# A second handover in each layer 1 step, and priority for the pre-pass softmax statistics

## The chip, the cores and the metric

The kernel runs on one core of one Trainium2 chip. The metric is the device time of one execution in microseconds; 4537.07 us is the median of three runs before the change (4530.45 to 4539.39). The core's engines each work through their own queue in order: TensorE (PE for matmuls, PEld for weight loads), VectorE (DVE), ScalarE (ACT), GpSimd (POOL) and SyncE (SP, which here only issues transfers).

## The reference

Four images of 32 x 32 positions and 384 channels pass through four layers; each adds its result to its input after a group normalisation (32 groups of 12 channels). N is 1024 positions.

```python
x = x + L0(_gn(x), ...)   # deformable attention, 6 heads of 64
x = x + L1(_gn(x), ...)   # attention with grouped weights, 12 heads of 32
x = x + L2(_gn(x))        # box sums over x and channels, a quotient
x = x + L3(_gn(x), ...)   # outlook attention, 3 x 3 windows

# L0: q = x @ w_q; offsets from a grouped 3 x 3 convolution of q, layer norm, gelu, tanh
xs = _bilinear_sample(xg, pos)                    # x at the offset positions
attn = softmax(einsum(q, xs @ w_k) * scale + bilinear(rpe, disp))
out = einsum(attn, xs @ w_v) @ w_out

# L1: per head, n and m over the 1024 positions
sim = sigmoid(beta + alpha * einsum('bhnd,bhmd->bhnm', l2norm(xg_h), l2norm(gc)))  # m: 256
group_weight = einsum('bhnm,bhkm->bhnk', sim, sim) * gamma + (1.0 - gamma)
attn = softmax(einsum('bhnd,bhmd->bhnm', q, k) * scale, axis=-1) * group_weight
attn = attn / (attn.sum(axis=2, keepdims=True) + 1e-08)      # sum over the rows n
out = einsum('bhnm,bhmd->bhnd', attn, v) @ Wproj
```

In layer 1 the softmax normalises over m and the second division sums over n. The kernel works on transposed scores, so it needs each row's logarithm of the softmax sum (maximum plus the log of the sum of exponentials) before it makes the scores. These logarithms come from a pre-pass.

## The kernel before

Two lanes of work are traced into one program. The trunk takes an image through layers 1, 2 and 3; the front takes the next image through layer 0. Both are Python generators that hand over with `yield w`, where w is a number of work units: 1109 for an image of the trunk, 714 for an image of the front. `Net.layer3` (L286) draws them: after each yield of the trunk it adds w / 1109 to what is done, and then draws from the front until the front is 0.1 of an image ahead. So a trunk yield of 14 draws 9.01 front units on the average, in whole pieces. Layer 0 of image 0 runs by itself ahead of this, and beside image 3 of the trunk no front is left.

The order in which the pieces are traced is a priority only. When the tile context closes, a scheduler goes through the program in modelled time, and whenever an engine is free it issues, of the instructions that are ready by its model, the one with the earliest place in the trace. `high_priority()` moves the places of what is traced inside it to the front, and `issue_after(ins)` keeps a block's instructions of one engine behind `ins`. The order on each engine is then fixed. On the chip an engine waits at its next instruction until that is ready, whatever stands behind.

**Layer 1 (trunk).** `inputs1` (L1198) makes the projections, the group convolution and the norms, and the pre-pass of head pair 0. Then `pair(p)` (L1463) handles six pairs of heads, each in eight steps j over 128 columns. A step scales a slice of sim on GpSimd (`sg`, L1513); makes the scores of 128 by 1024 for both heads in two double banks (L1530) and their exponentials (L1538, tiles `e`); then four products `product(h, r)`: the group weights of half h and head r, by transposing blocks that were kept from earlier steps (L1555) and by matmuls of sg and sim (L1560), multiplied into `e` with a running sum on VectorE (L1567), with a copy of the blocks wanted later (L1572). `values` (L1490), one step late, divides by the sums and adds to the value product `av` (L1502), a bank that is held for the whole pair. The first two or three products (`parts[:split]`) stand ahead of a piece of the next pair's pre-pass, the others behind.

**The pre-pass.** `sums_step(i, st)` (L1388) multiplies queries by keys into two double banks (L1397), takes the negative maximum on VectorE (L1405) and the exponential with its sum on ScalarE (L1406). Eight such steps make a pair's statistics; `sums_log` (L1414) turns them into the logarithm with two Newton steps (L1423 to L1429), and `sums_row` (L1432) transposes it (L1436) and stores it. In a pair's step the pre-pass matmuls stand behind the last product's matmul by `issue_after`.

**Layer 0 (front).** For each of six heads and two halves of the queries, `head0` (L831) has four key pairs (`yield 6` each): gathers of bias windows by GpSimd transfers (L845), interpolation on ScalarE and VectorE (L857, L858, L862, L863), two logits matmuls into two banks (L869), their sum with the bias (L872) and a running maximum (L874, L876). Then the maximum is transposed, reduced and spread (L883 to L895, `yield 3`), and eight keys follow in four pairs (`yield 2` each): subtraction (L902), exponential (L903), and matmuls with the values and with ones (L905). A copy and a store end the half (`yield 3`), and `over_sums` (L1127) divides after every second head.

All PSUM tiles come from two pools: `ps2` with two double banks (`big`), used by scores, pre-pass and sims, and `ps1` with four banks (`bank`), used by products, values, logits and the attention sums of layer 0.

Of the kernel before, what the change touches and what calls it, by code (L numbers as in the profile page):

```python
# [19 lines left out]
I32 = mybir.dt.int32  # L20
AF = mybir.ActivationFunctionType
ALU = mybir.AluOpType
AX = mybir.AxisListType
# [1127 lines left out]
class Trunk(Lane):  # L1151
# [236 lines left out]
    def sums_step(self, i, st):  # L1388

        nc, v = self.nc, self.nc.vector  # L1390
        nmax, den = st
        ps = [self.big() for _ in range(2)]
        for h in range(2):
            for r in range(2):
                c = 2 * h + r
                rows = slice(HD1 * c, HD1 * (c + 1))
                nc.tensor.matmul(  # L1397
                    ps[r][:, h * 512 : (h + 1) * 512],
                    self.q4[rows, i * P : (i + 1) * P],
                    self.k4[rows, 0:512],  # L1400
                    start=True,
                    stop=True,
                )
        for r in range(2):
            v.tensor_reduce(nmax[:, r, i : i + 1], ps[r], AX.X, ALU.max, negate=True)  # L1405
            nc.scalar.activation(  # L1406
                ps[r],
                ps[r],
                AF.Exp,
                bias=nmax[:, r, i : i + 1],  # L1410
                accum_out=den[:, r, i : i + 1],
            )

    def sums_log(self, st):  # L1414

        nc, v = self.nc, self.nc.vector
        nmax, den = st


        d = self.wt([P, 2, NJ], "dsum")  # L1420
        e = self.wt([P, 2, NJ], "dexp")
        ln2 = float(np.log(2.0))
        v.tensor_copy(d, den.bitcast(I32))  # L1423
        v.tensor_scalar(d, d, ln2 / 2**23, -(127.0 - 0.043) * ln2, ALU.mult, ALU.add)
        for _ in range(2):
            nc.scalar.activation(e, d, AF.Exp, scale=-1.0)
            v.tensor_tensor(e, e, den, ALU.mult)
            v.scalar_tensor_tensor(d, e, -1.0, d, ALU.add, ALU.add)
        v.tensor_tensor(d, nmax, d, ALU.subtract)  # L1429
        return d  # L1430

    def sums_row(self, p, d):  # L1432
# [30 lines left out]
    def pair(self, p):  # L1463
# [3 lines left out]
        nc, v = self.nc, self.nc.vector  # L1467
# [22 lines left out]
        def values(j, es, tot):  # L1490

            rt = self.wt([P, 2], "rt", 2)
            v.scalar_tensor_tensor(rt, tot[:, :, 0], 1e-8, tot[:, :, 1], ALU.add, ALU.add)
            v.reciprocal(rt, rt)
            vs = self.wt([P, 2, HD1], "vs", 2)
            v.tensor_tensor(  # L1496
                vs, vn[:, j].rearrange("p (r c) -> p r c", r=2), bc(rt, 2, HD1), ALU.mult
            )
            for h in range(2):
                for r in range(2):  # L1500
                    r0 = HD1 * (2 * h + r)
                    nc.tensor.matmul(  # L1502
                        av[r0 : r0 + HD1, :],
                        vs[:, r, :],
                        es[h][:, r, :],
                        start=j == 0,
                        stop=j == NJ - 1,
                    )

        for j in range(NJ):  # L1510
# [14 lines left out]
            for h in range(2):  # L1525
                cols = slice(h * 512, (h + 1) * 512)
                ps = self.big().rearrange("p (r n) -> p r n", r=2)
# [9 lines left out]
                e = self.wt([P, 2, 512], "e", 4)  # L1537
# [41 lines left out]
            with self.tc.issue_after(last):  # L1579
                if st and j < 2:  # L1580
                    self.sums_step(2 * j, st)
                elif st and j < 6:
                    self.sums_step(j + 2, st)
                elif st and j == 6:
                    self.sums_row(p + 1, logs)
                    self.load_lse(p + 1)
                    self.sims(0)
            for h, r in parts[split:]:
                last = product(h, r)
            with self.tc.issue_after(last):  # L1590
# [7 lines left out]
            if st and j == 5:  # L1598
                logs = self.sums_log(st)
                if p + 2 < NH1 // 2:  # L1600
                    self.load_sums(p + 2)
            yield 14
        values(*late.pop())
        y = self.wt([P, 512], "y")
        nc.scalar.copy(y, av)
# [357 lines left out]
```

## Time and profile before

| what | value |
|---|---|
| median of three runs | 4537.07 us (4530.45 to 4539.39) |
| profiled execution, its own time | 4529.22 us |
| its span, first to last instruction | 4527.0 us |
| mean granted TensorE clock | 0.932 |
| TensorE matmuls busy | 4011.3 us, 89% |
| VectorE / ScalarE / GpSimd busy | 3128.7 / 2308.8 / 960.1 us |
| pre-pass maximum, L1405 | 384 of 1219 ns |
| pre-pass exponential, L1406 | 384 of 1089 ns |
| product on VectorE, L1567 | 768 of 748 ns |

Times within the trace are microseconds from the start of the span. Each group line gives the busy time and the mean duration of one instruction, then the idle time of the engine ahead of it and what ended that. A waits line such as "PE bank L869 <- ACT gn L1572" says that TensorE stood still at line 869, which writes a tile `bank`, until ScalarE's instruction of line 1572 was done; the numbers are the total, the count and the longest. A row of the windows view has the stretch, its length, the busy time of PE, PEld, DVE, ACT and POOL with instruction counts, the granted clock, the share of the DMA engines and GB/s. A row of the timeline has start, duration, engine, line and operation.

By the trace, image 0's layer 0 runs up to about 560 us. The pair stages of images 0 to 3 lie at about 812 to 1440, 1916 to 2545, 3022 to 3658 and 3930 to 4310 us.

### The profile page before, as it was taken

To read this page: it belongs to the slowest core of one execution; us is meant where nothing else is said; L and a number is where in the kernel's file an instruction comes from. 1 tells how busy PE (TensorE), PEld (TensorE's weight loads), DVE (VectorE), ACT (ScalarE), POOL (GpSimd) and SP (SyncE) were. 2 spreads that over 40 slices of the span, in tenths; PEclk is the share of its full clock that TensorE was granted. 3 is DMA by queue.
4 is the path that set the end of the run, shared out by engine and by line. 5 is a ranking of instruction groups with operands and counts; after the bars stand their busy time and mean duration, and the time that the engine had idled before them with its cause. 6 is when DMAs were issued, how large, how long until landed. Compare 5 with 4: busy or idle time off the path is not lost.

```text
span 4527.0 us, 47048 instructions
## 1 busy us (share of the span) xinstructions
PE 4011.3 (89%) x15672; PEld 1702.4 (38%) x15672; DVE 3128.7 (69%) x5925; ACT 2308.8 (51%) x3633; POOL 960.1 (21%) x970
## 2 busy tenths in 40 slices
PE   5589889989899897998899989789999998999998
PEld 2222334333334443333333344343333334344444
DVE  3599566878887627677888744667788874566654
ACT  2176334666665323556766423456566651466632
POOL 0655123212121104211212110422121311000000
PEclk8799998999999898999999989898999998999998
DMA  7445344222222255312222135431122213311011
GB/s 153 146 148 145 100 129 120 75 57 77 62 66 63 82 134 151 111 48 58 85 58 82 38 95 154 143 107 51 45 78 58 78 38 115 121 29 37 22 41 42
DMA packets 298322, 389.85 MB, mean 86 GB/s; under 512 B 167875, under 2 KB 229664, under 8 KB 298080
## 3 DMA queue, kind: packets, MB, share of 16 engines
q1 hardware_dynamic: 246040, 220.14, 17.8%
q0 software_dynamic: 39936, 145.53, 10.9%
q10 hardware_dynamic: 12104, 21.19, 1.4%
q8 instruction: 124, 2.03, 0.2%
q14 instruction: 118, 0.97, 0.1%
HBM read 300.48 MB, written 86.56 MB: 85 GB/s over the span
## 4 chain that ended last, share of the span: by engine, by line
PE 57%; DVE 20%; issue 8%; ACT 5%; DMA 5%; POOL 3%; SPq 1%; another core or an unknown queue 0%; ACTq 0%; DVEq 0%; POOLq 0%
PE bank L1560 12%; PE big L1530 6%; PE big L400 5%; PE bank L905 4%; PE bank L414 4%; PE big L1397 4%; PE bank L1502 3%; DVE nmax L1405 3%; PE bank L1555 2%; PE bank L869 2%; DVE e L1567 2%; PE big L665 2%; DVE lg L872 2%; PE bank L1235 2%; PE big L1700 2%
## 5 line engine op out<-in xcount | busy, mean ns | idle before, releaser
L1560 PE MATMUL bank<-whole,sg 128*128 128x512 f32 (+3 forms) x2304 | 838.5, 497 | 0.0
L1567 DVE SCALAR_TENSOR_TENSOR e<-bank,gam,e 128x512 f32<-128x512 f32 x768 | 560.3, 748 | 298.6 <-PE bank L1560 146.8
L1406 ACT ACTIVATE big<-big,nmax 128x1024 f32<-128x1024 f32 x384 | 418.2, 1089 | 283.7 <-DVE nmax L1405 275.5
L1538 ACT ACTIVATE e<-big 128x1024 f32<-128x1024 f32 x384 | 380.5, 1020 | 289.3 <-PE big L1530 283.3
L1560 PEld LDWEIGHTS bank<-whole,sg 128*128 128x128 f32 x2304 | 396.3, 194 | 342.6 <-issue 254.3
L1405 DVE TENSOR_REDUCE nmax<-big 128x1 f32<-128x1024 f32 x384 | 453.1, 1219 | 85.7 <-PE big L1397 51.2
L1530 PE MATMUL big<-qa,ka 64*128 64x512 f32 x1536 | 463.2, 653 | 28.0 <-ACT big L1406 27.1
L845 POOL DMA_INDIRECT win<-strips,widx x288 | 326.8, 1135 | 714.6 <-DVE z L858 346.7
L1513 POOL TENSOR_SCALAR sg<-whole,gam 128x512 f32<-128x512 f32 x192 | 146.9, 766 | 1303.6 <-PE bank L1560 1029.0
L1397 PE MATMUL big<-k,q 32*128 32x512 f32 x1536 | 289.4, 662 | 47.7 <-ACT big L1406 35.0
L737 POOL DMA_INDIRECT gat<-pairs,sidx x192 | 207.8, 1082 | 408.1 <-DVE ix_gt L515 209.0
L905 PE MATMUL bank<-lg,va 128*64 128x512 f32 x576 | 271.3, 618 | 20.8 <-ACT lg L903 20.7
L905 PE MATMUL bank<-lg,ones 128*64 128x512 f32 x576 | 270.7, 618 | 0.0
L1530 PEld LDWEIGHTS big<-qa,ka 64*128 64x128 f32 x1536 | 164.3, 197 | 262.5 <-issue 111.3
L863 DVE SCALAR_TENSOR_TENSOR lg<-z,bias_f,lg 128x512 f32<-128x512 f32 x288 | 219.6, 778 | 62.4 <-ACT lg L862 58.4
L1502 PE MATMUL bank<-e,vs 128*32 128x512 f32 x1536 | 239.5, 632 | 6.6 <-DVE vs L1496 6.5
L857 ACT ACTIVATE z<-win,bias_f 128x528 f32<-128x528 f32 x288 | 204.5, 738 | 51.0 <-DMA win<-strips,widx 26.7
L858 DVE SCALAR_TENSOR_TENSOR z<-win,bias_f,z 128x528 f32<-128x528 f32 x288 | 216.7, 770 | 8.9 <-issue 4.6
L872 DVE TENSOR_TENSOR lg<-bank,lg 128x512 f32<-128x512 f32 x288 | 192.5, 684 | 35.4 <-PE bank L869 35.4
L862 ACT ACTIVATE lg<-z,bias_f 128x512 f32<-128x512 f32 x288 | 201.0, 719 | 18.4 <-DVE z L858 10.3
L902 DVE TENSOR_TENSOR lg<-lg,tb 128x512 f32<-128x512 f32 x288 | 183.8, 694 | 38.1 <-ACT tb L895 38.1
L903 ACT ACTIVATE lg<-lg 128x512 f32<-128x512 f32 x288 | 170.6, 628 | 44.8 <-DVE lg L902 41.6
(314 smaller groups left out, 6673.5 us busy)
## 6 DMA issues: line engine op xcount, KB each, us to landing
pairs<-xn SPq DMA_DIRECT2D x64, 192.0 KB
q<-qd SPq DMA_DIRECT2D x48, 256.0 KB
xg<-xgd SPq DMA_DIRECT2D x48, 256.0 KB
w<-in_gmat SPq DMA_DIRECT2D x16, 576.0 KB
w<-in_w_off SPq DMA_DIRECT2D x12, 576.0 KB
w<-in_Wqkv SPq DMA_DIRECT2D x12, 576.0 KB
a<-in_x SPq DMA_DIRECT2D x16, 384.0 KB
x<-a ACTq DMA_DIRECT2D x4, 1536.0 KB
```

The source lines that it names most:

```text
L400: nc.tensor.matmul(ps[:, h * 512 : (h + 1) * 512], w[:, ki, lo + ko * P : lo + (ko + 1) * P], mov, start=ki == 0, stop=ki == KC - 1,)
L845: nc.gpsimd.indirect_dma_start(out=win, out_offset=None, in_=self.strips[:, :], in_offset=bass.IndirectOffsetOnAxis(ap=self.widx[:, q, c : ...
L872: v.tensor_tensor(lf, ps[u], lf, ALU.add)
L905: nc.tensor.matmul(po[out, :], w, lf, start=j == 0, stop=j == NJ - 1)
L1397: nc.tensor.matmul(ps[r][:, h * 512 : (h + 1) * 512], self.q4[rows, i * P : (i + 1) * P], self.k4[rows, 0:512], start=True, stop=True,)
L1405: v.tensor_reduce(nmax[:, r, i : i + 1], ps[r], AX.X, ALU.max, negate=True)
L1406: nc.scalar.activation(ps[r], ps[r], AF.Exp, bias=nmax[:, r, i : i + 1], accum_out=den[:, r, i : i + 1],)
L1502: nc.tensor.matmul(av[r0 : r0 + HD1, :], vs[:, r, :], es[h][:, r, :], start=j == 0, stop=j == NJ - 1,)
L1530: nc.tensor.matmul(ps[:, r, :], ka[rows, j * P : (j + 1) * P], qa[rows, cols], start=True, stop=True,)
L1538: nc.scalar.activation(e, ps, AF.Exp)
L1560: last = nc.tensor.matmul(ps[:, (mid - i0) * P :], sg[:, r, m, :], sim[:, h, r, m, (mid - i0) * P :], start=m == 0, stop=m == 1,)
L1567: v.scalar_tensor_tensor(e[:, r, :], ps, self.gam[:, 1:2], e[:, r, :], ALU.add, ALU.mult, accum_out=tot[:, r, h : h + 1],)
```

## The change

Each step of `pair` yields 7 units twice in place of 14 once. The new yield stands behind the first products and the pre-pass piece that follows them, ahead of the remaining products. The pre-pass maximum and exponential of `sums_step` and all of `sums_log` are traced under `high_priority()`; the pre-pass matmuls are not. The instructions are the same.

```diff
         for r in range(2):
-            v.tensor_reduce(nmax[:, r, i : i + 1], ps[r], AX.X, ALU.max, negate=True)
-            nc.scalar.activation(
-                ps[r],
-                ps[r],
-                AF.Exp,
-                bias=nmax[:, r, i : i + 1],
-                accum_out=den[:, r, i : i + 1],
-            )
+            with self.tc.high_priority():
+                v.tensor_reduce(nmax[:, r, i : i + 1], ps[r], AX.X, ALU.max, negate=True)
+                nc.scalar.activation(
+                    ps[r],
+                    ps[r],
+                    AF.Exp,
+                    bias=nmax[:, r, i : i + 1],
+                    accum_out=den[:, r, i : i + 1],
+                )
...
-        v.tensor_copy(d, den.bitcast(I32))
-        v.tensor_scalar(d, d, ln2 / 2**23, -(127.0 - 0.043) * ln2, ALU.mult, ALU.add)
-        for _ in range(2):
-            nc.scalar.activation(e, d, AF.Exp, scale=-1.0)
-            v.tensor_tensor(e, e, den, ALU.mult)
-            v.scalar_tensor_tensor(d, e, -1.0, d, ALU.add, ALU.add)
-        v.tensor_tensor(d, nmax, d, ALU.subtract)
+        with self.tc.high_priority():
+            v.tensor_copy(d, den.bitcast(I32))
+            v.tensor_scalar(d, d, ln2 / 2**23, -(127.0 - 0.043) * ln2, ALU.mult, ALU.add)
+            for _ in range(2):
+                nc.scalar.activation(e, d, AF.Exp, scale=-1.0)
+                v.tensor_tensor(e, e, den, ALU.mult)
+                v.scalar_tensor_tensor(d, e, -1.0, d, ALU.add, ALU.add)
+            v.tensor_tensor(d, nmax, d, ALU.subtract)
         return d
...
+            yield 7
             for h, r in parts[split:]:
                 last = product(h, r)
             with self.tc.issue_after(last):
...
-            yield 14
+            yield 7
         values(*late.pop())
```

## The prediction

> **What bounds the kernel now.** I read the page from the top: the span and the busy shares, then the forty slices, then single stages in the windows view, then TensorE's waits in one stage, and last the timeline at one wait.
>
> ```profile
> span 4527.0 us, 47048 instructions
> PE 4011.3 (89%) x15672; PEld 1702.4 (38%) x15672; DVE 3128.7 (69%) x5925; ACT 2308.8 (51%) x3633; POOL 960.1 (21%) x970
> PE   5589889989899897998899989789999998999998
> DVE  3599566878887627677888744667788874566654
> PEclk8799998999999898999999989898999998999998
> ```
>
> TensorE is the bound, 89% of the span over all. The windows view sets the pair stage of images 0, 1 and 2, which runs beside layer 0 of the next image, against that of image 3, which runs alone (last line):
>
> ```profile
> 812.00:1440.00 628.00, 573.17 (x2415) 231.10 (x2417) 510.46 (x1017) 399.04 (x634) 133.00 (x130) 0.96 0.23 65
> 1916.00:2545.00 629.00, 573.89 (x2413) 230.94 (x2409) 510.56 (x1016) 399.41 (x634) 132.50 (x130) 0.96 0.23 65
> 3022.00:3658.00 636.00, 583.16 (x2419) 234.60 (x2415) 511.37 (x1017) 399.11 (x634) 131.62 (x130) 0.94 0.23 65
> 3930.00:4310.00 380.00, 375.15 (x1757) 156.88 (x1755) 246.88 (x560) 238.63 (x377) 28.12 (x40) 1.00 0.13 34
> ```
>
> Alone, TensorE idles 4.9 of 380 us at full clock. Beside layer 0 it idles 55.1 of 629 us (54.8 and 52.8 in the other two) at a mean clock of 0.94 to 0.96, while VectorE is 81% busy. All that the change can win is in these three stretches and the stage ahead of each. Who holds TensorE there (image 1, pair stage and the run-in; total, times, longest):
>
> ```profile
> PE bank L883 <- DVE rmax L876: 11.4, 8, 1.7
> PE big L1530 <- ACT big L1406: 8.5, 3, 3.2
> PE big L1397 <- ACT big L1406: 6.5, 4, 2.7
> PE bank L1555 <- DVE lg L872: 5.2, 6, 2.1
> PE bank L869 <- ACT gn L1572: 5.0, 3, 3.6
> PE bank L905 <- ACT lg L903: 4.5, 3, 2.1
> PE bank L869 <- DVE lg L872: 3.9, 4, 2.7
> ```
>
> Two causes stand out. One is the pre-pass (L1406): its two double banks are all that the scores also use. The timeline shows why it is late; the product L1397 ends at 1980.67, its maximum starts only at 1983.62, behind layer 0's L858 and L863:
>
> ```profile
> 1978.36 2.31 PE L1397 MATMUL big<-k,q 32*128 32x512 f32 x8
> 1980.14 1.45 DVE L858 SCALAR_TENSOR_TENSOR z<-win,bias_f,z 128x528 f32<-128x528 f32 x2
> 1982.29 1.42 DVE L863 SCALAR_TENSOR_TENSOR lg<-z,bias_f,lg 128x512 f32<-128x512 f32 x2
> 1983.62 2.35 DVE L1405 TENSOR_REDUCE nmax<-big 128x1 f32<-128x1024 f32 x2
> 1986.94 3.18 PE L1397 MATMUL big<-k,q 32*128 32x512 f32 x8 [2.64 <-ACT big L1406]
> ```
>
> The other is layer 0's seam L876, L883, where its running maximum is turned. And a stall costs twice; in the windows behind the one above the clock (third column from the end) is halved for 6.83 us, then whole again:
>
> ```profile
> 1986.35:1993.18 6.83, 6.24 (x20) 1.97 (x21) 6.05 (x12) 4.40 (x9) 4.59 (x4) 0.50 0.29 91
> 1993.18:2000.01 6.83, 6.83 (x30) 3.41 (x32) 5.62 (x10) 2.84 (x5) 0.00 (x0) 1.00 0.17 47
> ```
>
> **The change part by part.** No instruction is added or removed; the scheduler's order changes.
>
> *A, priority of maximum and exponential.* In image 1 (1860 to 2545 us) I read off the timeline, for each of the pre-pass steps, the time from the end of L1397 to the start of L1405: 14 of 36 wait over 0.6 us, 35.8 us together, longest 5.21. TensorE's waits that follow are 8.5 + 6.5 for L1406, and the 3.6 of L869 behind the copy L1572, which stood behind two exponentials: 18.6 us, so 0.52 us of stall per us of delay. Near them lie 23.9 us at half clock, worth up to 12 us; 0.64 us per us of stall. With priority the maximum waits only for the instruction under way (about 0.4 us), and the 18.6 us should go. What is late next is the VectorE work passed by: 14 times two reduces of 1.22 us, 34 us. Of the 60 instructions ahead of the late maxima, 13 are the trunk's own L1567, which free banks; 47 are layer 0's. If only the trunk's hurt, at the same 0.52, 3.9 us come back; if all do, 17.8. I take the middle, 10.8, since layer 0's L902 feeds L905, whose wait is in the list above, while L858 only fills logits tiles ahead of need. Net 7.8 us, 12.8 with the clock, 38 over three images. Ends: 18.6 x 1.64 x 3 = 92 won; all 34 us come back, 15.6 x 1.64 x 3 = 77 lost. ScalarE is 63% busy here and I cost its reordering within these ends.
>
> The clock's share can be weighed against the Trainium skill, "TensorE: Matmul & The Clock Gate", section "HAM oscillation", which says that only idle gaps over about 3.4 us throttle. By that rule no stall of this stage but the 3.6 us one would cost clock; the row above (0.50 after 2.64 us) says otherwise, and the sum goes by the row.
>
> *B, the seam.* Counting both generators' yields: a step of 14 trunk units draws 9.01 of layer 0 (14 x 714 / 1109). A key pair's block is 6 (call it L), the turn of the maximum 3 (X), a pair of exponentials with L905 2 (A). Before, 6 of an image's 7 X came in one handover right behind their last L, and 11 times two L came together; with 4.5 units per half step neither happens at all. Half a step of trunk matmuls (629 / 48 = 13.1 us a step) then stands between L876 and L883. Reach: 11.4 us x 6/7, with 6.8 us of clock likewise, 15.6 us an image, 47 in all. I take half, 23, because the scheduler places by readiness and not by trace order alone. Against it, 26 of the 38 A now come half a step nearer to X; L905's wait was 2.07 us each time, and two more of them per image cost 12 (ends 0 and six, 37). Net 11 won.
>
> *C, the mid-step blocks.* 27 of the 44 L in an image's pair stage move ahead of the step's last one or two products. An L holds two of four banks until L872, and the value product holds one throughout, so the products behind it share one. TensorE's waits behind L872 are 3.9 + 5.2 us per image now, 0.21 per L; I charge that again for the 27: 17 in all. Ends: nothing, and a whole L1567 and copy (0.75 + 0.37 us) each time, 27 x 1.12 x 3 = 91. I stay near the row that shows the same wait at its present place.
>
> *The queues.* Each moved L carries two POOL gathers (L845), four ScalarE scalings and two key loads per head on SP. The next step's L1513 stands behind both handovers before and after, so POOL's order to the trunk is kept, and POOL is 21% busy there. On SP the blocks of j = 5, with the sums' loads and stores of layer 0, move ahead of the four loads of load_sums; these are wanted two steps, 26 us, later. Nothing is charged; without that slack a rden load (4.2 us in the chain) would be the price.
>
> *D, the logarithm.* Its tiny chain (0.17 us each) makes TensorE wait 5.7 + 3.4 us at L1436 over 24 pairs; I take 4 back.
>
> *E, the stage before the pairs.* The pre-pass of pair 0 stands behind layer 0's gather weights (L750), with TensorE waiting 5.3 + 1.1 us for L1406 an image: up to 19 to win. Pushing L753 back by three steps of 2.44 us would cost as much at L764: 22. I take nothing.
>
> Image 3 has no layer 0 left and its maxima start 0.04 us after their products: nothing. Sum: -38 - 11 + 17 - 4 = -36. The profiled execution took 4529.2 us (span 4527.0 and 2.2 around it), so 4493; the median of the runs shown is 7.9 above it, so 4501.
>
> **The rivals.**
>
> *The banks decide (slower).* C at its upper end, 91 in place of 17: -38 - 11 - 4 + 91 = +38, 4575. It turns from 0.65 us per moved block on. For it: the 3.6 us wait at L869 was one for a bank. Against it: single waits behind L872 are rarely over 1 us. Beside it, the same sign by another place: *the passed VectorE work comes back in full*, decided where over 0.54 us returns per us passed; at 0.7, 18.6 - 23.9 = -5.3, +26, and with the rest 4565. Its measured neighbour, 0.52, is close, which is why I don't give it little. Together 0.28.
>
> *The priority moves nothing.* The scheduler may hold the product for unfinished where the hardware has it done, and then no maximum is ready to go ahead. A and D are nothing, -11 + 17 = +6: 4543, within what can be told. Speaking for it: nothing in the trace shows what the scheduler believed. Against: L902, three in a row, is all ready at once, and the maximum stands behind it in six of the 14. 0.10.
>
> *Stalls vanish without a return.* A at 92, B at 47, D at 9 and C at 17: 4406; half way there 4454. For it: image 3. Against: VectorE's 81%. 0.08.
>
> *Idle costs no clock.* A 23, B 15 less 12, C 17, D 4: -13, 4524. The rows at 0.50 speak against it. 0.04. By the rule of the Trainium skill above this would be the time.
>
> **How the numbers follow.** The forecast keeps 0.50 (4470 to 4527 by itself). A measurement of this kernel tells 0.2% (9 us; its three runs lie 8.9 apart). Faster: 0.50 + 0.08 + 0.04 = 0.62; same 0.10; slower 0.28. The range runs from 4445, which leaves out part of the no-return case, to 4572, which takes in the returned work and stops just short of the banks' end.
>
> **What would show it.** A right: the gap from L1397 to L1405 falls under 0.5 us beside layer 0, and "L1397 <- L1406" and "L1530 <- L1406" nearly go from TensorE's waits. B right: "L883 <- L876" falls to a few us an image. C: waits of L1555, L1560 or L869 for L872 and L1567 grow by about 6 us an image. D: L1436 no longer waits for L1429. The pair windows' idle goes from 55 to some 45 us and the clock toward 0.98. It would be wrong if L1567 and L902, passed by, left TensorE as idle as before under other names, or if the mid-step blocks starve the products of banks.

## The result and the profile after

The changed kernel takes 4498.34 us (median of six runs, 4493.76 to 4509.69), the kernel before 4533.61 us on the same chip: a ratio of 0.993, 95% interval 0.9913 to 0.9947. The forecast was 4501 us. The number came out; most of the working behind it did not.

The page of the changed kernel, in the lines shown of before (its profiled execution took 4504.37 us, mean clock 0.937 after 0.932):

```profile
span 4502.6 us, 47093 instructions
PE 3953.3 (88%) x15672; PEld 1661.2 (37%) x15672; DVE 3108.4 (69%) x5925; ACT 2305.0 (51%) x3633; POOL 949.3 (21%) x970
PE   5589898898989798899899989798989998999998
PEclk8799998999999898999999989899999998999998
```

TensorE is busy 58 us less, with the same number of instructions, in a span that is 24.4 us shorter. So it stands still longer than before and yet finishes earlier. The prediction had said that its idle time would go.

The windows view, with the whole pair stage of images 0 to 2 (first to last score product) in a row each. Before:

```profile
713.00:1431.00 718.00, 659.61 (x2687) 267.24 (x2687) 567.60 (x1106) 450.06 (x718) 157.89 (x155) 0.96 0.24 69
1818.00:2537.00 719.00, 657.29 (x2690) 266.54 (x2689) 569.48 (x1108) 450.94 (x718) 155.75 (x153) 0.96 0.25 70
2921.00:3647.00 726.00, 666.28 (x2688) 270.10 (x2686) 569.31 (x1106) 450.65 (x718) 157.83 (x155) 0.95 0.25 69
```

and after:

```profile
725.00:1435.00 710.00, 642.33 (x2689) 255.01 (x2688) 565.28 (x1112) 450.61 (x719) 153.10 (x155) 0.97 0.25 70
1814.00:2534.00 720.00, 656.14 (x2686) 260.00 (x2685) 565.03 (x1112) 450.12 (x718) 151.12 (x152) 0.95 0.24 68
2916.00:3627.00 711.00, 642.18 (x2687) 254.74 (x2686) 564.60 (x1112) 449.19 (x719) 149.91 (x152) 0.97 0.24 69
```

To a tenth, the three stages beside layer 0 took 718.0, 718.7 and 725.8 us before and now take 709.5, 720.4 and 711.3. That is 21.3 of the 24.4 us. Image 3, alone, is as it was (443.0, now 442.7). Idle in the three grew from 58.4, 61.7 and 59.7 us to 67.7, 63.9 and 68.8, while time at half clock fell from 61.6, 58.0 and 78.7 us to 44.9, 72.8 and 42.7. Image 1 has more half-clock time than before, and it is the one stage that gained nothing.

TensorE's waits in the pair stage of image 1 (lines from L1405 on stand one or two lower down in this kernel: L1405 is L1406, L1406 is L1407, L1496 is L1498, L1502 is L1504, L1530 is L1532, L1555 is L1557, L1567 is L1569):

```profile
PE big L1532 <- ACT big L1407: 24.6, 12, 5.1
PE bank L891 <- POOL diag L889: 7.8, 9, 1.3
PE bank L1557 <- DVE lg L872: 5.5, 5, 2.3
PE bank L1504 <- DVE vs L1498: 5.5, 5, 1.9
PE bank L869 <- DVE e L1569: 5.1, 5, 2.2
...
PE bank L883 <- DVE rmax L876: 1.7, 2, 1.4
```

The seam L883 went from 11.4 to 1.7 us. But the wait that the priority was to remove did not go: 8.5 us at the scores and 6.5 at the pre-pass products became 24.6 at the scores. The page's groups show the other half of it. Before:

```profile
L1530 PE MATMUL big<-qa,ka 64*128 64x512 f32 x1536 | 463.2, 653 | 28.0 <-ACT big L1406 27.1 <-issue 0.3
L1397 PE MATMUL big<-k,q 32*128 32x512 f32 x1536 | 289.4, 662 | 47.7 <-ACT big L1406 35.0 <-ACT e L1538 8.5 <-issue 3.8
L1502 PE MATMUL bank<-e,vs 128*32 128x512 f32 x1536 | 239.5, 632 | 6.6 <-DVE vs L1496 6.5
```

and after:

```profile
L1532 PE MATMUL big<-qa,ka 64*128 64x512 f32 x1536 | 453.0, 672 | 84.2 <-ACT big L1407 79.3 <-ACT e L1540 2.2 <-issue 1.6
L1397 PE MATMUL big<-k,q 32*128 32x512 f32 x1536 | 263.8, 658 | 65.2 <-ACT big L1407 48.4 <-ACT e L1540 11.8 <-issue 4.9
L1504 PE MATMUL bank<-e,vs 128*32 128x512 f32 x1536 | 207.9, 608 | 18.2 <-DVE vs L1498 18.2
```

The scores wait 79.3 us in place of 27.1. The value products take 207.9 us busy in place of 239.5, and the pre-pass products 263.8 in place of 289.4, at nearly the same mean duration of one. Such products run side by side, so busy time that falls at an equal mean means that more of them overlap.

Why did the priority not pull the maximum forward? The timeline of the changed kernel at its longest wait, the 5.09 us one:

```profile
2212.56 1.14 PE L1397 MATMUL big<-k,q 32*128 32x512 f32 x8
...
2213.55 0.08 DVE L1569 DVE_READ_ACCUMULATOR e<-bank,gam,e 128x1 f32 x1
2214.50 1.13 DVE L863 SCALAR_TENSOR_TENSOR lg<-z,bias_f,lg 128x512 f32<-128x512 f32 x1 [0.87 <-issue]
2215.55 0.76 DVE L858 SCALAR_TENSOR_TENSOR z<-win,bias_f,z 128x528 f32<-128x528 f32 x1
2216.23 0.74 DVE L1569 SCALAR_TENSOR_TENSOR e<-bank,gam,e 128x512 f32<-128x512 f32 x1
...
2218.39 0.74 DVE L858 SCALAR_TENSOR_TENSOR z<-win,bias_f,z 128x528 f32<-128x528 f32 x1
2219.06 2.34 DVE L1406 TENSOR_REDUCE nmax<-big 128x1 f32<-128x1024 f32 x2
...
2221.56 1.23 PE L1532 MATMUL big<-qa,ka 64*128 64x512 f32 x2 [5.09 <-ACT big L1407]
```

The product is done at 2213.70. VectorE stands idle for 0.87 us until 2214.50, and L863, L858, the trunk's L1569 and more go first; the maximum, which has the priority, starts 5.36 us after its product. VectorE's 5157 instructions start in this trace in exactly the order in which the program queues them, so the maximum's place was set by the scheduler. Over the 40 pre-pass steps of image 1's stage the mean gap from product to maximum rose from 0.96 to 1.22 us, and 19 of them wait over 0.6 us where 14 did.

The gap alone doesn't make the longer wait, though. Here is a step in which the maximum is prompt, 0.47 us after its product (2108.79):

```profile
2107.65 1.14 PE L1397 MATMUL big<-k,q 32*128 32x512 f32 x8
...
2108.72 1.07 PE L1504 MATMUL bank<-e,vs 128*32 128x512 f32 x8
...
2109.26 2.35 DVE L1406 TENSOR_REDUCE nmax<-big 128x1 f32<-128x1024 f32 x2
...
2111.83 1.83 PE L1532 MATMUL big<-qa,ka 64*128 64x512 f32 x6 [0.98 <-ACT big L1407]
```

From the start of the maximum to the scores it takes 2.57 us, for one maximum and one exponential, and TensorE had only 2.06 us of other work. So such a wait is the gap plus about 2.6 us, less the work that TensorE has between the pre-pass product and the scores. For the 12 waits in image 1's stage that is 27.6 + 30.8 - 33.4 = 25.0 us, and 24.6 were measured; for the three of before, 12.2 + 7.7 - 11.1 = 8.8 against 8.5. Before, each of the 40 steps had at least 2.6 us of work there; now 7 have less. That, besides the longer gaps, is why the wait grew.

### The profile page after: what moved, and what is told of

It reads as the page before. It is cut to its first block, busy times and chain, and to the rows that moved or that the text cites. A ratio compares the mean times of both kernels' runs of the same rounds, so it can differ in the third digit from the quotient of the medians.

```text
span 4502.6 us, 47093 instructions
## 1 busy us (share of the span) xinstructions
PE 3953.3 (88%) x15672; PEld 1661.2 (37%) x15672; DVE 3108.4 (69%) x5925; ACT 2305.0 (51%) x3633; POOL 949.3 (21%) x970
## 3 DMA queue, kind: packets, MB, share of 16 engines
q0 software_dynamic: 39936, 145.53, 10.8%
## 4 chain that ended last, share of the span: by engine, by line
PE 53%; DVE 22%; issue 9%; ACT 7%; DMA 4%; POOL 3%; SPq 1%; another core or an unknown queue 1%; ACTq 0%; DVEq 0%; POOLq 0%
PE bank L1562 11%; PE big L1532 6%; PE big L400 5%; PE bank L905 4%; DVE nmax L1406 4%; PE bank L414 4%; PE big L1397 3%; DVE e L1569 3%; ACT big L1407 3%; PE bank L1557 2%; PE big L665 2%; PE bank L1235 2%; PE bank L1504 2%; PE bank L869 2%; DVE lg L872 2%
## 5 line engine op out<-in xcount | busy, mean ns | idle before, releaser
L1562 PE MATMUL bank<-whole,sg 128*128 128x512 f32 (+3 forms) x2304 | 853.9, 501 | 1.5
L1569 DVE SCALAR_TENSOR_TENSOR e<-bank,gam,e 128x512 f32<-128x512 f32 x768 | 560.3, 746 | 314.2 <-PE bank L1562 184.8
L1407 ACT ACTIVATE big<-big,nmax 128x1024 f32<-128x1024 f32 x384 | 417.5, 1087 | 316.9 <-DVE nmax L1406 289.4
L1532 PE MATMUL big<-qa,ka 64*128 64x512 f32 x1536 | 453.0, 672 | 84.2 <-ACT big L1407 79.3
L1406 DVE TENSOR_REDUCE nmax<-big 128x1 f32<-128x1024 f32 x384 | 451.9, 1216 | 77.3 <-PE big L1397 60.7
L845 POOL DMA_INDIRECT win<-strips,widx x288 | 313.9, 1090 | 691.6 <-DVE z L858 367.0
L1397 PE MATMUL big<-k,q 32*128 32x512 f32 x1536 | 263.8, 658 | 65.2 <-ACT big L1407 48.4
L905 PE MATMUL bank<-lg,va 128*64 128x512 f32 x576 | 268.3, 606 | 13.6 <-ACT lg L903 13.6
L1532 PEld LDWEIGHTS big<-qa,ka 64*128 64x128 f32 x1536 | 148.1, 198 | 343.4 <-ACT big L1407 173.1
L905 PE MATMUL bank<-lg,ones 128*64 128x512 f32 x576 | 267.7, 606 | 0.0
L863 DVE SCALAR_TENSOR_TENSOR lg<-z,bias_f,lg 128x512 f32<-128x512 f32 x288 | 216.0, 767 | 47.5 <-ACT lg L862 44.5
L857 ACT ACTIVATE z<-win,bias_f 128x528 f32<-128x528 f32 x288 | 205.4, 736 | 60.5 <-DVE lg L863 31.4
L858 DVE SCALAR_TENSOR_TENSOR z<-win,bias_f,z 128x528 f32<-128x528 f32 x288 | 213.9, 760 | 17.1 <-ACT z L857 9.2
L1504 PE MATMUL bank<-e,vs 128*32 128x512 f32 x1536 | 207.9, 608 | 18.2 <-DVE vs L1498 18.2
L1574 ACT COPY gn<-bank 128x128 f32<-128x128 f32 (+2 forms) x288 | 106.1, 369 | 195.8 <-DVE e L1569 192.5
L872 DVE TENSOR_TENSOR lg<-bank,lg 128x512 f32<-128x512 f32 x288 | 191.1, 681 | 9.9 <-PE bank L869 9.1
```

What stands on the lines that cost most here:

```text
L845: nc.gpsimd.indirect_dma_start(out=win, out_offset=None, in_=self.strips[:, :], in_offset=bass.IndirectOffsetOnAxis(ap=self.widx[:, q, c : ...
L872: v.tensor_tensor(lf, ps[u], lf, ALU.add)
L905: nc.tensor.matmul(po[out, :], w, lf, start=j == 0, stop=j == NJ - 1)
L1397: nc.tensor.matmul(ps[r][:, h * 512 : (h + 1) * 512], self.q4[rows, i * P : (i + 1) * P], self.k4[rows, 0:512], start=True, stop=True,)
L1407: nc.scalar.activation(ps[r], ps[r], AF.Exp, bias=nmax[:, r, i : i + 1], accum_out=den[:, r, i : i + 1],)
L1504: nc.tensor.matmul(av[r0 : r0 + HD1, :], vs[:, r, :], es[h][:, r, :], start=j == 0, stop=j == NJ - 1,)
```

## The experiments

Each ratio is to the kernel before on the same chip, with its 95% interval. The four chips used here give 4499 to 4506 us for the kernel before, 28 to 35 us less than the chip of the result, so only ratios are compared. The table takes the means over the three pair stages beside layer 0, in us per image. "Half lost" is half of TensorE's busy time at half clock, that is, what the clock costs; the columns of products are their share of TensorE's time, brought to full clock. "Torn" counts, in TensorE's order over the whole program, the groups of four value products (L1502) that have other work in between.

| kernel | ratio | length | idle | half lost | values | pre-pass | scores | torn |
|---|---|---|---|---|---|---|---|---|
| before | 1 | 720.9 | 59.9 | 32.5 | 52.5 | 55.4 | 95.2 | 21 |
| after | 0.9930 | 713.7 | 66.8 | 25.4 | 46.9 | 49.9 | 98.5 | 3 |
| e1_split | 0.9929 | 712.5 | 69.6 | 21.3 | 46.9 | 50.5 | 98.7 | 3 |
| e2_prio | 0.9987 | 721.1 | 59.8 | 31.9 | 52.3 | 55.5 | 95.8 | 21 |
| e5_apart | 0.9994 | 722.3 | 64.0 | 34.6 | 50.7 | 53.1 | 92.8 | 15 |
| e6_glued | 1.0039 | 735.4 | 85.0 | 30.3 | 46.9 | 49.7 | 98.9 | 6 |
| e7_behind | 1.0439 | 786.5 | 104.3 | 53.5 | 47.2 | 43.9 | 104.8 | 3 |
| e8_four | 0.9967 | 716.7 | 60.6 | 20.1 | 47.7 | 49.2 | 103.6 | 9 |
| e9_ahead | 1.0093 | 738.1 | 77.2 | 28.4 | 56.5 | 51.0 | 99.9 | 36 |
| e10_sooner | 1.0110 | 736.1 | 65.3 | 33.5 | 48.7 | 58.7 | 100.1 | 9 |
| e11_whole | 1.0066 | 728.8 | 66.8 | 42.1 | 45.6 | 54.1 | 95.6 | 0 |
| e12_split_whole | 0.9934 | 714.0 | 68.3 | 25.7 | 45.9 | 50.0 | 98.9 | 0 |
| e13_endearly | 0.9988 | 720.2 | 62.1 | 24.7 | 47.7 | 51.4 | 104.7 | 6 |
| e14_filler | 0.9990 | 717.9 | 54.3 | 24.2 | 48.7 | 55.0 | 98.0 | 9 |

### The two parts apart: the second handover alone (e1_split), the priority alone (e2_prio)

```diff
 e1_split, to the kernel before
+            yield 7
             for h, r in parts[split:]:
...
-            yield 14
+            yield 7
```

> The second handover alone, no priority. Theory S (the handover carries all of the gain, since the priority hardly moves an instruction beside layer 0): ratio to before 0.993, within 0.3% of the changed kernel; TensorE's waits at L883 about 2 to 3 us per image, those for L1406 about 25 us per image. Rival P (priority and handover each give a part, as the prediction's sum had it: 38 and 11 less 17): about 1.001, within 0.3% of before.

```diff
 e2_prio, to the kernel before
         for r in range(2):
+            with self.tc.high_priority():
                 v.tensor_reduce(...)
                 nc.scalar.activation(...)
...
+        with self.tc.high_priority():
             v.tensor_copy(d, den.bitcast(I32))
...
```

> The priority alone, one handover of 14. Theory S: within 0.2% of before, and the gap between the pre-pass product and its maximum stays at 0.96 us on the average in the pair stage, 14 of 40 steps over 0.6 us. Rival P: ratio 0.991 and a gap under 0.5 us.

The handover alone gives 4466.2 against 4502.61 us, 0.9929 (0.9917 to 0.9942): all of the gain. Of image 1's waits with it (those for the seam fall, those for the pre-pass rise, as in the changed kernel):

```profile
PE big L1530 <- ACT big L1406: 25.6, 12, 4.8
...
PE bank L883 <- DVE rmax L876: 3.3, 2, 2.0
```

The priority alone gives 4491.7, 0.9987 (0.9974 to 1.0), which is within 0.2% of before, as expected. Beside layer 0 it changes next to nothing; image 1's waits with the priority alone:

```profile
PE bank L883 <- DVE rmax L876: 11.4, 8, 1.7
PE big L1532 <- ACT big L1407: 7.7, 3, 3.2
...
PE big L1397 <- ACT big L1407: 5.9, 4, 2.6
...
PE bank L869 <- ACT gn L1574: 5.0, 3, 3.6
```

These are nearly the rows of before (11.4, 8.5, 6.5, 5.0). So are the gaps: mean 0.95 us, 15 steps over 0.6. The static order tells the same: the priority moves 30 of 8882 instructions of TensorE, 48 of 5159 of VectorE and 15 of 3324 of ScalarE, all of them in the stages ahead of the pairs; the handover moves 2373, 1701 and 990. So the rival "the priority moves nothing" held for step A. A likely reason is that there was nothing for it to choose: while the scheduler does not hold the product for done, as the 0.87 us of idle VectorE above suggests, a place at the front is of no use. What the scheduler believed is inferred from the order alone and is in no trace.

### Is the order behind the maximum the reason? (e7_behind)

If late maxima were the loss, an order that forces them forward should win. On top of e1_split, VectorE's work of the second half of a step, layer 0's pieces included, is queued behind the maxima of the middle pre-pass piece; the other engines' queues are not tied:

```diff
+            self.top = v.tensor_reduce(nmax[:, r, i : i + 1], ps[r], ...).ins
...
-            yield 7
-            for h, r in parts[split:]:
-                last = product(h, r)
+            if st and j < 6:
+                with self.tc.issue_after(self.top):
+                    yield 7
+                    for h, r in parts[split:]:
+                        last = product(h, r)
+            else:
+                yield 7
+                ...
```

> The second handover without priority, and in the five steps with a pre-pass all VectorE work traced at the middle (layer 0's and the last products') is queued behind the step's maxima. Theory L (the late maxima make the 25 us per image of scores waiting for pre-pass banks, and bringing them forward wins): mean gap from product to maximum falls from 1.26 to under 0.8 us, these waits to under 15 us, ratio to before 0.988 to 0.991. Rival D (the work passed by comes back as waits of TensorE under other names): the waits for L1406 fall, others grow as much, ratio 0.992 to 0.996.

4702.72 us, 1.0439 (1.0415 to 1.0462), far above both expected ranges. The gaps did fall, to a mean of 0.69 us, with 10 steps over 0.6. The waits of image 1:

```profile
PE big L1530 <- ACT big L1406: 26.4, 14, 3.9
PE bank L1555 <- DVE lg L872: 14.9, 8, 6.4
PE bank L905 <- ACT lg L903: 14.2, 8, 4.3
PE bank L1502 <- DVE vs L1496: 11.2, 9, 1.8
```

The scores wait for the pre-pass as long as in e1_split (25.6), and the work that was passed comes back at three other places. So earlier maxima, got at this price, do not even shorten the wait behind L1406 that they were to remove. The sum from above says why: 14 waits with gaps of 21.7 us in all, and only 31.2 us of TensorE's work between products and scores (none at all in three of them), make 26.5 us, for the 26.4 measured. The edit holds back more than the work ahead of the maxima, so it does not say what a cheaper way to earlier maxima would bring; it does say that the stall does not follow the gap alone.

### Is it the parted seam? (e5_apart, e6_glued)

Step B said that the running maximum L876 and its turn L883 no longer fall into one handover. e5_apart does only that: the step keeps its one handover, but drawing stops after the last key pair of a half. e6_glued does the opposite on top of e1_split: two handovers, with the turn always drawn together with the last key pair.

```diff
 e5_apart, to the kernel before
-                self.ahead += next(self.fronts, FRONT_STEPS) / FRONT_STEPS
+                step = next(self.fronts, FRONT_STEPS)
+                self.ahead += int(step) / FRONT_STEPS
+                if step == 6.5:
+                    break
...
-                yield 6
+                yield 6.5 if j == NJ - 1 else 6
```

> One handover of 14 as before, no priority, but the drawing stops after the last key pair of a head's half, so that the turn of its maximum comes one whole step later. Seam theory (the gain is the turn no longer standing right behind its last key pair): L883's wait falls from 11 to 2 us per image and most of the gain is there, ratio 0.994 to 0.996. Rival, even spreading (the gain is that the rest of layer 0 is drawn in smaller pieces): ratio 0.998 to 1.002, even if L883's wait falls.

```diff
 e6_glued, to e1_split
-                yield 6
+                yield 0 if j == NJ - 1 else 6
...
-        yield 3
+        yield 9
```

> Two handovers of 7, no priority, but the turn always comes in the same handover as its last key pair. Seam theory: L883's wait is back at 10 us per image or above, and the ratio back at 0.998 to 1.002. Even spreading: L883's wait is back, yet the ratio stays at 0.993 to 0.996.

e5_apart takes 0.9994 (0.9984 to 1.0003), e6_glued 1.0039 (1.0026 to 1.0052). The rows of e5_apart, image 1 (L886 is the seam there, L1558 is L1555, L875 is L872):

```profile
PE bank L1558 <- DVE lg L875: 9.9, 6, 4.8
...
PE bank L886 <- DVE rmax L879: 6.4, 4, 1.7
```

and of e6_glued:

```profile
PE big L1530 <- ACT big L1406: 24.8, 17, 4.0
...
PE bank L883 <- DVE rmax L876: 9.5, 8, 1.4
```

Parting the seam inside a single handover only halves its wait (the expectation had 2 us), and 4.7 us more of waiting appear where products want a bank behind L872 (9.9 after 5.2 us); the kernel is no faster. Glueing it with two handovers brings the seam's wait back, to 9.5 us, and the kernel is slower than both expectations had it, by 1.1% against e1_split. But glueing also makes one portion of nine units, so this does not part the seam from the size of the portions. What the two runs show is that parting by itself, which halves the wait, is worth nothing, and that the second handover gains nothing when it draws the turn together with the last key pair.

### How fine, and where? (e8_four, e9_ahead, e13_endearly, e10_sooner)

All stand on e1_split. e8_four hands over four times 3.5 units; e9_ahead has the first handover ahead of the products; e13_endearly has the second one ahead of `values`; e10_sooner keeps the handovers and puts the pre-pass piece behind the first product.

```diff
 e8_four: yield 3.5 at four places
             for h, r in parts[:split]:
                 last = product(h, r)
+                if (h, r) == (0, 0):
+                    yield 3.5
...
-            yield 7
+            yield 3.5
             for h, r in parts[split:]:
                 last = product(h, r)
+            yield 3.5
...
 e9_ahead
+            yield 7
             for h, r in parts[:split]:
                 last = product(h, r)
...
-            yield 7
             for h, r in parts[split:]:
...
 e13_endearly
+            yield 7
             if late:
                 values(*late.pop())
...
-            yield 7
         values(*late.pop())
...
 e10_sooner
-            for h, r in parts[:split]:
-                last = product(h, r)
-            with self.tc.issue_after(last):
+            first = product(*parts[0])
+            with self.tc.issue_after(first):
...
+            for h, r in parts[1:split]:
+                last = product(h, r)
             yield 7
```

> Four handovers of 3.5 per step, no priority. Even spreading (smaller pieces of layer 0 are what wins): better than two, ratio 0.988 to 0.991. Rival, place (only a handover at that one place helps, by what it leaves together in TensorE's queue): 0.994 to 1.000; 9 of the value products' groups of four are torn in place of 3.

> Two handovers of 7, no priority, the first ahead of the step's products in place of behind the pre-pass. The turn of the maximum is parted from its last key pair here too. Even spreading: ratio 0.991 to 0.995 as with the changed kernel. Place and packing: 36 groups of the value products are torn into one and three (before 21, changed 3), some 8 us of TensorE per image more than in the changed kernel, ratio 0.998 to 1.006.

> Two handovers of 7, the first in the changed kernel's place, the second ahead of the value products in place of behind them; no priority. The seam is parted as in the changed kernel, 3 score groups more are torn and no value group is torn into one and three. Even spreading: 0.991 to 0.995. Place (each shift of a handover may lose what it wins): 0.996 to 1.005, with more waits at L1502 or L1555.

> The second handover without priority, and the pre-pass product queued behind the first product of the step in place of the second or third, so that its double banks are filled one or two products sooner. Theory L: the scores of the next step wait less for the pre-pass banks, under 12 us per image in place of 25, ratio 0.985 to 0.990. Rival B (the pre-pass then waits for the banks that the exponentials of the scores hold, and the maxima go ahead of products that free the small banks): waits of L1397 for L1538 grow by 5 us or more per image, ratio 0.993 to 1.002.

Measured: e8_four 0.9967 (0.9954 to 0.998), e9_ahead 1.0093 (1.0073 to 1.0113), e13_endearly 0.9988 (0.9976 to 1.0001), e10_sooner 1.011 (1.0093 to 1.0127). The first and third lie where the rival of place had them; e9_ahead and e10_sooner are slower than any expectation. Portions as even as in e1_split win 0.7% at one place and lose 0.9% at another, so evenness by itself isn't the cause. In e9_ahead the products of the same step wait for the banks of the key pairs that now stand right ahead of them, as step C had feared:

```profile
PE bank L1555 <- DVE lg L872: 21.0, 16, 3.6
```

and its value products are torn most often, 36 times. Four portions have the least half-clock loss (20.1) and an idle time as before (60.6), but the scores are spread out by pieces in between (103.6 us per image for 95.2) and eat most of it. In e13_endearly the scores do the same (104.7). In e10_sooner the early pre-pass products wait for the exponentials L1538 in turn (13.0 us in image 1 for e1_split's 4.7), and take 58.7 us where e1_split takes 50.5.

### Is it the torn groups? (e11_whole, e12_split_whole)

The table's column "values" follows its column "torn": 21 torn groups less 3 and 52.5 less 46.9 us in each of three images make 0.93 us a group; e9_ahead's 33 more than e1_split's make 0.87. The timeline of before shows one, beside the next seam:

```profile
2272.19 0.63 PE L883 MATMUL bank<-ident,rmax 128*128 128x128 f32 x4 [1.21 <-DVE rmax L876]
2272.75 1.12 PE L1530 MATMUL big<-qa,ka 64*128 64x512 f32 x2
2273.80 1.04 PE L1502 MATMUL bank<-e,vs 128*32 128x512 f32 x2
...
2281.48 1.06 PE L1502 MATMUL bank<-e,vs 128*32 128x512 f32 x6
```

The first of the four products (two records) takes 1.04 us by itself, and the other three take 1.06 together, which is also what all four take when nothing is in between. (The Trainium skill, "TensorE: Matmul & The Clock Gate", section "Part 3: Packing small matmuls", has it that products that use only 32 columns of the array can run in it at the same time, at different tile positions; the 1.06 us for four and 1.04 for one agree.) Both kernels keep the groups whole; layer 0 has no hand in it:

```diff
             if late:
-                values(*late.pop())
+                with self.tc.issue_after(last):
+                    values(*late.pop())
```

> The kernel before, with the four value products of a step queued behind its last group-weight matmul, so that none of the 21 torn groups (one and three) is left; 30 TensorE instructions move. Packing theory (a torn group costs TensorE about 0.9 us, as the value products' time over the runs so far has it): value products from 52.5 to about 46 us per image, the stage some 5 us shorter, ratio 0.996 to 0.998. Rival (what tears the group is useful work that fills the gap, so nothing is won): value products shorter, but the stage within 2 us and the ratio 0.998 to 1.002.

> The second handover alone, with the value products queued in the same way (3 torn groups to 0). Both theories: within 0.2% of the second handover alone, ratio 0.991 to 0.994; it is tried as the better version.

On the kernel before (e11_whole) the values fall to 45.6 us as reckoned, 6.9 us less per image, and the kernel gets slower: 1.0066 (1.0048 to 1.0085). No expectation had that. Here is where image 1 loses it:

```profile
PE bank L883 <- DVE rmax L876: 14.1, 9, 3.2
PE bank L891 <- POOL diag L889: 9.1, 10, 2.3
```

The lone value product had stood in a wait at the seam (11.4 and 4.6 us there before). With it gone the wait is longer; an image's stage idles 6.9 us more, and time at half clock in the three stages goes from 198 us to 273. On top of the handover (e12_split_whole), where hardly any group is torn, it changes nothing: 0.9934 (0.9915 to 0.9953). No kernel here is faster than e1_split by more than can be told.

### Is it the clock? (e14_filler)

To pay for the clock alone, the kernel before gets one product of 128 x 512 whose result nobody reads, ahead of each turn of the maximum and into the bank that the turn then overwrites. It needs only an earlier key pair's logits, so it can run in the wait for L876:

```diff
         ps = self.bank()
+        nc.tensor.matmul(ps, self.ident, logits[NJ - 2], start=True, stop=True)
         for i in range(NI):
             nc.tensor.transpose(
```

> The kernel before, with one matmul more of 128 by 512 (0.86 us) at each of the 36 seams of layer 0, into the bank that the transposes then overwrite, so that TensorE works for part of the time in which it stood still there; its order is otherwise nearly that of before. Nothing in it needs the maximum, so no wait is shortened by it. Clock theory (what a seam costs is as much the half clock that follows as the standing itself): the half clock of the three stages falls from about 200 us to 140 or less, the waits at L883 shorten to under 0.5 us each, and the ratio is 0.993 to 0.998 in spite of 31 us of added work. Rival (only the standing counts): ratio 1.000 to 1.007, whatever the clock does.

4496.23 us, 0.999 (0.9978 to 1.0001), between the two expected ranges, with 36 products and 45.2 us of TensorE's time added. The product does not cover the whole wait: in image 1 it waits 7.6 us itself, behind L872. The windows view of its three pair stages:

```profile
709.00:1426.00 717.00, 661.35 (x2708) 266.01 (x2709) 567.40 (x1108) 448.29 (x718) 154.88 (x155) 0.97 0.25 70
1801.00:2518.00 717.00, 663.24 (x2711) 266.67 (x2710) 567.67 (x1108) 448.49 (x718) 155.96 (x156) 0.97 0.25 70
2893.00:3613.00 720.00, 666.49 (x2708) 268.30 (x2706) 567.42 (x1108) 448.13 (x719) 156.16 (x156) 0.96 0.25 70
```

They are 3.0 us shorter than before on the average (720.9 to 717.9), though each holds 11.0 us more of work at full clock (10.8 of filler; values lose 3.8 us as torn groups fall from 21 to 9, and scores and logits gain 4.0): 8.3 us come back from the clock and 5.6 from idle. Time at half clock in the three stages goes from 198 us before, and 208 in e2_prio, to 147; in the changed kernel it is 160, in e1_split 136. Of the 43 spells at half clock that begin in these stages before, 8 had the seam as the main wait in the 3.41 us in front of them; here none of 29 has. The mean clock of all its runs is 0.941 to 0.946, that of the runs of before beside them 0.931 to 0.938. So stalls at the seam do cost clock, and the cost is of the size that the handover saves (7.1 us an image after, 11.2 in e1_split). The total moved little, as the filler takes its own time: the experiment fixes the clock's part, not the whole.

## Why the prediction was right in its number and wrong in its working

The sum -38 - 11 + 17 - 4 = -36 stands against a measured 4498.34 - 4533.61 = -35. That the two meet is luck: without A the same terms make +2, a kernel that is no faster, while the handover alone gave -36 (4466.2 against 4502.61). Step by step:

**A, the priority, -38, failed.** The sentence that fell is "with priority the maximum waits only for the instruction under way (about 0.4 us), and the 18.6 us should go". The gaps hardly fell beside layer 0 (e2_prio: 0.96 to 0.95 us; the stage has 40 such steps, not the 36 that were counted), and the priority as a whole is worth 0.9987, at most 0.26% by its interval. The rival that says so got 0.10 and was right for A; what it lacked was a gain from somewhere else. The handover even made the waits for L1406 grow, from 15.0 us to 24.6 in image 1. And the factor of 0.52 us of stall per us of delay was no law: in e7_behind the gap is 0.69 us in place of 0.96, and the stall at L1530 is 26.4 us in place of 8.5. A stall is the delay plus 2.6 us less the work in between, and the handover changed that work.

**B, the seam, -11, right in mechanism and mis-sized.** The wait at L883 fell from 31.4 to 7.1 us over the three stages: 24.3 us, nearly the whole reach of 26.9 (six sevenths) and not half of it. The spells at half clock with that wait in front went from 44 us (102 in e2_prio's profile) to 3. The charge of 12 us for L905 is a term with the wrong sign: its wait fell, from 13.4 to 6.3 us over the three stages. What B did not say is that parting with one handover only halves the wait and pays nothing (e5_apart).

**C, the banks, +17, did not come.** Its sign was to be that the waits of L1555, L1560 and L869 for L872 and L1567 grow by about 6 us an image. Over the three stages they fell, from 36.9 us to 32.9. They changed names: in image 1, L869 now waits 5.1 us behind the trunk's L1567, where it waited 5.0 behind the copy L1572 and 3.9 behind L872. What did grow there stands in no step: L1502 behind L1496, 2.3 to 5.5 us, and L891 behind L889, 4.6 to 7.8. The mechanism of C shows where the handover stands ahead of the products (e9_ahead): 21.0 us in image 1.

**The queues, nothing charged, held:** no wait of TensorE for POOL's `sg` or for a load of the sums stands among image 1's.

**D, -4, wrong in sign.** TensorE's waits at L1436 were 9.1 us before, 5.7 of them behind L1429; they are 11.1 after, 3.1 of them behind L1429. The handover alone raises them to 21.1 (e1_split, most of it behind the trunk's own VectorE work), and with the priority beside it 10 us of that are gone again. No gain in time shows for it: 0.9930 with the priority, 0.9929 without. Per image the changed kernel idles 2.8 us less than e1_split and loses 4.1 more to the clock, in the one profile of each.

**E, taken as nothing, came out so in the sum.** Waits for L1406 ahead of the pairs grew from 13.6 us in all to 47.6, and e2_prio has 36.2, so here the priority does move something, to the worse for this wait. Yet the time outside the three pair stages did not grow (it is 3 us shorter), so another chain ends later there.

**Not foreseen at all** was that the handover changes how the same products lie in TensorE's queue. Per image of the three stages, at full clock: values -5.6, pre-pass -5.5, sims and layer 0's logits -2.0 each, scores +3.3, group weights +2.8; with the rest the work takes 7 us less. The pre-pass products are never torn by other work in either kernel; but 25 of their 120 steps before, and 12 after, start at a wait or are broken by one, and then take 2.1 to 2.3 us of TensorE where the others take 1.1 to 1.2. The clock loses 7 us less, idle time is 7 us more, and the stage is 7 us shorter. "The pair windows' idle goes from 55 to some 45 us" was therefore wrong in sign: idle rose by 7 us, and the clock of the three windows moved from 0.96, 0.96 and 0.95 to 0.97, 0.95 and 0.97, not "toward 0.98".

The rivals: *the banks decide* did not; *idle costs no clock* (4524 us, the time by the rule quoted from the Trainium skill) is refuted by e14_filler, where shortening stalls of 1 to 2 us took the half-clock time in the three stages down by a quarter.

So what is shown: the handover carries the gain; the gain goes when the turn is drawn with its last key pair (e6_glued), or when a handover stands at another place (e9_ahead, e13_endearly); the clock's part is real. That the packing of products contributes is argued from the work saved, 7 us an image, and not shown by the total: e11_whole saves 8.5 us of work and e6_glued 8.3, and both are slower than before, as idle time takes more. How the 7 us of fewer half-clock losses divide among single waits stays open, since a spell of half clock depends on where a stall falls on the clock's windows, and image 1 of the changed kernel (72.8 us) against its neighbours (44.9 and 42.7) shows how far that goes in one profile.

## What to carry to other kernels

By the scheduler's rule a priority only chooses among what its model holds for ready: before pricing one, look for the work that was passed over, and ask whether the marked instruction could have been known to be ready then. When two lanes of work are interleaved, try places and portions of the handover one by one, because the same portions won 0.7% at one place and lost 0.9% at another. Before pricing a late instruction, add up what the waiting engine has to do meanwhile: here a prompt maximum still stalled TensorE wherever less than 2.6 us of other work lay in between. And read TensorE's waits together with its clock and with how its small products pack: a kernel can idle longer and be faster, and a torn group can be the only thing that fills a wait.

## What the runs showed of the hardware

**The clock goes by windows, not by gaps.** Spells at half clock are whole multiples of 3.41 us on one grid through the run. With the profile of before cut on that grid, a window at full clock with TensorE busy under 0.4 of it is followed by one at half clock 56 times of 56; from 0.4 to 0.6 it is 17 of 43, from 0.6 to 0.8 14 of 85, above 0.8 1 of 961. At half clock, a window under 0.8 busy is followed by another 57 times of 57. A single stall of 1.72 us was enough here, at a seam of before (windows view; PE's busy time is the second number after the stretch, the clock the third from the end):

```profile
1945.40:1948.81 3.41, 1.69 (x13) 0.46 (x6) 3.12 (x5) 1.61 (x2) 0.00 (x0) 1.00 0.88 217
1948.81:1952.22 3.41, 3.41 (x9) 1.45 (x9) 0.69 (x1) 0.44 (x1) 1.04 (x1) 0.50 0.07 23
```

The free-running window agrees with the Trainium skill, "TensorE: Matmul & The Clock Gate", section "Part 1: The HAM clock gate"; the page's rule of thumb in "HAM oscillation", that only idle gaps over about 3.4 us throttle, does not fit these rows.

**A torn group of side-by-side products costs nearly a whole one:** 1.04 us for one of four, 1.06 for four, about 0.9 us per torn group over the kernels here. The same holds for a group that a wait breaks or delays: 2.1 to 2.3 us for a pre-pass step in place of 1.1 to 1.2.
